# A four-tap convolution over tokens, moved from VectorE to TensorE's diagonal matrices in the first image

## The chip, the core and the metric

The kernel runs on one core of a Trainium2 chip, in fp32 throughout. The metric is the device time of one execution in microseconds. A profile belongs to one execution of its own. Engines are named as the profile names them: PE is TensorE's matrix multiplication, PEld its weight load, DVE is VectorE, ACT is ScalarE, POOL is GpSimd, and SP is SyncE, which here issues most of the transfers.

## The reference, cut to what matters

Four images of 384 channels and 48 x 48 tokens pass through four layers with residuals: a Mamba block, a patch-wise frequency filter with a depthwise convolution, an 11 x 11 depthwise convolution, and a mixture of four experts. The change touches the first layer alone:

```python
xz = xs @ in_proj_w.T
xin, z = jnp.split(xz, 2, axis=-1)
xc = jnp.pad(xin.transpose(0, 2, 1), ((0, 0), (0, 0), (D_CONV - 1, 0)))   # D_CONV = 4
xc = jax.lax.conv_general_dilated(xc, conv_w[:, None, :], (1,), 'VALID', ...)  # one filter per channel
xin = jax.nn.silu((xc + conv_b[None, :, None]).transpose(0, 2, 1))
...
h_new = dA * h_prev + dBx        # for 768 channels x 16 states, token after token
y_t = jnp.einsum('bds,bs->bd', h_new, C_t)
```

Each of the 768 inner channels has its own four weights: a token's value is the weighted sum of itself and the three tokens before it. That sum, `xc`, is what the change makes in another way. The scan of `h_new` follows.

## The kernel before

**Chunks and slots.** An image's 2304 tokens are cut into five chunks of 460 or 464 tokens (0 to 4), and the 768 channels into six row tiles of 128 partitions. One chunk of scans is 96 slots: three pairs of row tiles, and in each pair 16 states for both tiles. In each slot POOL multiplies `u` and `B` into `bu` (L831), ACT makes the decay `da` as an exponential (L820), DVE runs the scan (L844), and the result is multiplied by `C`, by DVE in two slots of three (L864) and by POOL in the third (L873). PE transposes the product with the identity and sums it in a bank `y` (L770), ACT keeps the last column as `carry` (L858). Decays are made two slots ahead of their scan, `bu` three, in small buffers (two banks for `da`, three buffers for `bu`, six for `g`).

**The order of the work.** Each engine carries out its own instructions in the order in which they were written. That order is set when the kernel is built, by a planner in slots: every other piece of work of the first layer is a task, a generator that yields the engine it wants next, and `plan` gives each task the slot from which it may go (`put(45 + 3 * j, ("x", more, j), ...)` for the projections of the next chunk). A task moves on when its slot has come, its needs are ended and a bank of the ring of three PSUM banks (`ring`) is free. Nothing of this is decided on the chip, so an instruction that waits holds up all that stands behind it on its engine.

**The projection.** `project(i, j)` makes row tile `j` of the next chunk: PE multiplies three blocks of the input projection into a bank `pin` (L642), with three columns of tokens from the chunk before it ahead of its own (the halo). ACT writes `xc` from `pin`, with the fourth weight as scale and the bias `cb` (L655). DVE adds the other three taps from the bank in three instructions (L661), and the bank is released. `project_z` makes the gate's part `pinz` in the same manner (L674, ACT copy L682). `gates` waits for all six tiles of both, loads another activation table and applies the silu to the whole of `xc` and `zs` (L693, L696), loads the first table back (L548), and `expand` (`pdbl`, L708) follows on PE. `steps` makes the time steps (`pdt` L734, ACT L744 to L747, DVE L750).

**What lies around it.** In the slots of the first image only the first layer works. From the second image on, the later layers of the image before it are tasks of other lanes and fill PE and DVE too. Ahead of the slots stands a setup: constants and weights, group norm statistics of the first image, `fold` (ACT scales the projection's weights by the norm, L591; PE makes their bias, `pbias` L598), and the first chunk's projections.

Of the kernel before, what the change touches and what calls it, by code (L numbers as in the profile page):

```python
# [9 lines left out]
F32 = mybir.dt.float32  # L10
AF = mybir.ActivationFunctionType
# [5 lines left out]
P = 128  # L17
# [4 lines left out]
DI, DS, DTR, DCONV = 768, 16, 24, 4  # L22
MT = DI // P
CHUNKS = (460, 460, 460, 460, 464)
TM = max(CHUNKS)
# [108 lines left out]
def wait(slots):  # L134
    for _ in range(slots):
        yield ("pool",)
# [3 lines left out]
def tile_layers(ctx: ExitStack, tc: tile.TileContext, a: dict, out: bass.AP):  # L140
    nc = tc.nc
# [6 lines left out]
    def const(name, shape, src, eng=None):  # L148
        t = cp.tile(shape, F32, name=name)
        (eng or nc.sync).dma_start(t, src)  # L150
        return t

    def per_channel(ap):
        tail = "abcd"[: len(ap.shape) - 1]
        tail = " ".join(tail)
        return ap.rearrange(f"(m p) {tail} -> p m {tail}", p=P)
# [4 lines left out]
    ident = const("ident", [P, P], a["c_ident"])  # L161
# [251 lines left out]
    with ExitStack() as first:  # L413
# [4 lines left out]
        def weight(name, shape, src):  # L418
            t = wp.tile(shape, F32, name=name)
            nc.scalar.dma_start(t, src)  # L420
            return t
# [4 lines left out]
        conv_w = weight("conv_w", [P, MT, DCONV], per_channel(a["L0_conv_w"]))  # L426
# [45 lines left out]
        with (  # L472
# [4 lines left out]
            for ct in range(CT):  # L477
                t = pp.tile([P, HW], F32, name=f"x0_{ct}")
# [58 lines left out]
        NC = len(CHUNKS)  # L537
# [14 lines left out]
        def now(steps):  # L552
            for _ in steps:
                pass

        def scans(wk, mm, ring, meter, place, lanes, begin):
# [5 lines left out]
            LEN = PAIR * (MT // 2)  # L562
# [19 lines left out]
            def fold(b, which):  # L582
                w = (w_inx, w_inz)[which]
                d = batch[b]
                nc.sync.dma_start(
                    w, per_channel(a["L0_in_proj_wT"])[:, :, bass.ts(which, DI)]
                )
                yield from wait(5)
                for k in range(CT):
                    yield ("act",)  # L590
                    nc.scalar.activation(  # L591
                        w[:, k, :], w[:, k, :], AF.Copy, scale=rstd0[:, b, k : k + 1]
                    )
                yield ("pe", 0, (ring, 1))
                ps, r = ring.take(f"pbias{b}_{which}")
                for j in range(MT):
                    for k in range(CT):
                        nc.tensor.matmul(  # L598
                            ps[:, j : j + 1],
                            lhsT=w[:, k, bass.ts(j, P)],  # L600
                            rhs=mean0[:, b, k : k + 1],
                            start=k == 0,
                            stop=k == CT - 1,
                        )
                yield ("dve",)
                nwm = d["nwm", which] = small.tile(
                    [P, MT], F32, name=f"nwm{b}_{which}", tag=f"nwm{which}"
                )
                nc.vector.tensor_scalar_mul(nwm, ps[:, :MT], -1.0)
                if which == 0:  # L610
                    wm = d["wm"] = small.tile([P, MT], F32, name=f"wm{b}", tag="wm")
                    nc.vector.tensor_copy(wm, ps[:, :MT])
                    cb = d["cb"] = small.tile([P, MT], F32, name=f"cb{b}", tag="cb")
                    nc.vector.tensor_tensor(cb, conv_s, nwm, ALU.mult)
                    nc.vector.tensor_tensor(cb, cb, conv_b, ALU.add)
                ring.done(r)
# [14 lines left out]
            def project(i, j):  # L631

                (b, t), c = G[i], st[i]
                n, d = CHUNKS[t], batch[b]
                halo = DCONV - 1
                lo = 0 if t else halo
                yield ("pe", 2.3, (ring, 1))
                if "xc" not in c:
                    c["xc"] = wk.tile([P, MT, TM], F32, name=f"xc{b}_{t}", tag="xc")
                ps, r = ring.take(f"pin{b}_{t}_{j}")  # L640
                for k in range(CT):
                    nc.tensor.matmul(  # L642
                        ps[:, lo : halo + n],
                        lhsT=w_inx[:, k, bass.ts(j, P)],
                        rhs=c["x"][:, k, lo : halo + n],
                        start=k == 0,
                        stop=k == CT - 1,
                    )
                yield ("act",)
                if t == 0:  # L650
                    nc.scalar.activation(
                        ps[:, :halo], nil[:, :halo], AF.Identity, bias=d["wm"][:, j : j + 1]
                    )
                acc = c["xc"][:, j, :n]
                nc.scalar.activation(  # L655
                    acc, ps[:, halo : halo + n], AF.Identity,
                    bias=d["cb"][:, j : j + 1], scale=conv_w[:, j, halo : halo + 1],
                )
                yield ("dve",)
                for k in range(halo):  # L660
                    nc.vector.scalar_tensor_tensor(  # L661
                        acc, ps[:, k : k + n], conv_w[:, j, k : k + 1], acc, ALU.mult, ALU.add
                    )
                ring.done(r)
# [159 lines left out]
            def drive(u):  # L824
                i, p, m, s, _ = where(u)
                (b, t), c = G[i], st[i]
                n = CHUNKS[t]
                bu = live["bu", u] = wk.tile(
                    [P, TM], F32, name=f"bu{b}_{t}_{m}_{s}", tag="bu", bufs=3
                )  # L830
                nc.gpsimd.tensor_mul(  # L831
                    bu[:, :n], c["u", p][:, m % 2, :n], live["B", u // 2][:, :n]
                )
# [139 lines left out]
                nc.sync.dma_start(x1d[b][bass.ts(ct, P), bass.ds(starts[t], n)], x)  # L973

            aux = Lane(1 << 30, meter, bound=False)
            named = {}

            def plan(i, at):
# [58 lines left out]
            def ready(u):  # L1037
# [3 lines left out]
                while task and not task.ended:  # L1041
# [3 lines left out]
                    n += 1  # L1045
                    assert n < 1000, "stuck"

            now(fold(0, 0))
            now(fold(0, 1))
            now(load(0))  # L1050
            for j in range(MT):
                now(project(0, j))
# [4 lines left out]
            with tc.manual_schedule():  # L1057
                ordered[0] = True
                for k in range(3):
                    spread(k, 0)  # L1060
                    spread(k, 1)
                for u in range(3):
                    drive(u)
                spread(3, 0)
                for u in range(2):
                    decay(u)
                for u in range(N + 6):
                    if u % LEN == 0 and u <= N:
                        plan(u // LEN, u)
                    if u < N and u % (LEN * NC) == 42 and u > 42:  # L1070
                        begin(G[u // LEN][0])
                    place[0] = u
                    for lane in (aux, *lanes):
                        lane.step(True, u)
                    for h, e in ((1, u - 4), (0, u - 5)):
                        if 0 < e < N and e % PAIR == PAIR - 1:
                            collect(e, h)
                    if u < N:
                        scan(u)


                    meter.slot(0.44)
                    early = u % PAIR >= 8
                    if early:
                        add(u - 5, True)
                        add(u - 3, False)
                    for lane in (aux, *lanes):
                        lane.step(False, u)
                    if u < N:
                        product_now(u)  # L1090
                    if u + 2 < N:
                        decay(u + 2)
                    if 0 < u <= N:
                        product(u - 1)
                    if u + 3 < N:
                        ready(u + 3)
                        drive(u + 3)
                    if not early:
                        add(u - 5, True)
                        add(u - 3, False)  # L1100
                    if u % 2:
                        spread((u + 7) // 2, 0)
                        spread((u + 5) // 2, 1)

                at = u
                while aux.queue or aux.active:
                    at += 1
                    meter.slot(0.0)
                    for act in (True, False):
                        for lane in (aux, *lanes):  # L1110
                            lane.step(act, at)
                lanes[0].drain(at, lanes[1:])
                place[0] = at
                ordered[0] = False
# [653 lines left out]
        ring, accr = psum("mm", 3), psum("acc", 1)  # L1768
# [167 lines left out]
```

## Time and profile before

| what | value |
|---|---|
| time, median of 3 runs | 5467.04 us (5466.89 to 5471.5) |
| the profiled execution's own time | 5472.59 us |
| its span | 5470.3 us |
| granted TensorE clock, mean | 0.912 |
| busy over the span: PE | 4689.8 us (86%) |
| DVE | 4176.4 us (76%) |
| ACT | 2999.9 us (55%) |
| POOL | 3124.6 us (57%) |
| L642 `pin`, PE, whole span | 720 records, 332.5 us |
| L844 scans, DVE, row with 1008 records | 1182.5 us, 1173 ns each |

A row of the profile names a line, an engine, an operation, what it writes and reads, its count and its busy time; then the time the engine sat idle just before it and what ended that wait. The shares are means over the whole span, in which stages with different limits follow each other: the slots of the first image fill about the first fifth, and from about 4600 us on PE works nearly alone. In a timeline a line begins with the start and the duration in microseconds. Durations of instructions that follow each other overlap by a little, so what a group costs its engine is read from start to start.

### The profile page before, as it was taken

How to read it: one execution, taken by the hardware profiler on the slowest of the kernel's cores; microseconds unless marked ns; L12 is line 12 of the kernel's file. 1: busy time of each engine (PE TensorE's matmuls, PEld its weight loads, DVE VectorE, ACT ScalarE, POOL GpSimd, SP SyncE). 2: the span in 40 equal slices, each digit the busy share in tenths (PEclk: the TensorE clock that was granted, in tenths of full speed). 3: DMA queues.
4: the chain of work that ended last, by engine and by line, in shares of the span. 5: the costliest groups of instructions: out<-in, count | busy, mean ns of one | idle time of the engine just before them, and what ended most of it. 6: DMA issues, size and time to landing. Idle time of an engine off the chain costs nothing. (4 is left out here: it accounts for less than half of the span.)

```text
span 5470.3 us, 82006 instructions
## 1 busy us (share of the span) xinstructions
PE 4689.8 (86%) x27796; PEld 3688.4 (67%) x27796; DVE 4176.4 (76%) x5806; ACT 2999.9 (55%) x6632; POOL 3124.6 (57%) x2795
## 2 busy tenths in 40 slices
PE   5677677777678989988899999988899999999899
PEld 3445445454447767665678887665678878888799
DVE  5889989999898898899988788899988774443200
ACT  3555555565458765655467655665566753334321
POOL 3878878865567777665567667665666662000000
PEclk8788888798789999999899999999999999999899
DMA  4445445454345555544566566554556564543200
GB/s 121 135 137 147 124 128 146 128 149 124 104 125 148 151 160 163 172 140 140 152 169 174 155 166 175 153 154 130 164 158 169 163 175 145 148 138 102 66 27 23
DMA packets 628393, 758.97 MB, mean 139 GB/s; under 512 B 58869, under 2 KB 622181, under 8 KB 627582
## 3 DMA queue, kind: packets, MB, share of 16 engines
q1 hardware_dynamic: 617668, 751.98, 48.5%
q8 instruction: 221, 3.62, 0.3%
q10 hardware_dynamic: 10298, 1.67, 0.2%
q14 instruction: 206, 1.69, 0.1%
HBM read 663.81 MB, written 89.65 MB: 138 GB/s over the span
## 5 line engine op out<-in xcount | busy, mean ns | idle before, releaser
L831 POOL TENSOR_TENSOR bu<-u,B 128x460 f32<-128x460 f32 (+1 forms) x1920 | 2226.4, 1168 | 1118.2 <-DVE g L844 506.7
L820 ACT ACTIVATE da<-dt,a_neg 128x460 f32<-128x460 f32 (+1 forms) x1920 | 1243.7, 649 | 317.3 <-DVE g L864 223.0
L770 PE MATMUL y<-ident,g 128*115 128x128 f32 (+1 forms) x7680 | 1169.0, 295 | 273.4 <-DVE g L864 202.0
L770 PEld LDWEIGHTS y<-ident,g 128*115 128x115 f32 (+1 forms) x7680 | 1024.1, 185 | 546.9 <-DVE g L864 246.8
L844 DVE TENSOR_TENSOR_SCAN da<-da,carry,bu 128x460 f32<-128x460 f32 (+1 forms) x1008 | 1182.5, 1173 | 69.9 <-ACT da L820 48.7
L873 POOL TENSOR_TENSOR g<-g,C 128x460 f32<-128x460 f32 (+1 forms) x660 | 767.7, 1163 | 197.9 <-ACT carry L858 195.9
L864 DVE TENSOR_TENSOR g<-da,C 128x460 f32<-128x460 f32 (+1 forms) x1260 | 796.4, 632 | 87.1 <-DMA C<-bcd 28.1
L844 DVE TENSOR_TENSOR_SCAN g<-da,carry,bu 128x460 f32<-128x460 f32 (+1 forms) x528 | 616.8, 1168 | 105.6 <-ACT da L820 61.1
L858 ACT COPY carry<-da 128x1 f32<-128x1 f32 x1008 | 159.0, 158 | 948.1 <-DVE g L864 944.8
L1601 PE MATMUL pout<-hr,we 128*128 128x144 f32 x3456 | 488.9, 298 | 49.7 <-ACT hr L1617 30.5
L1601 PEld LDWEIGHTS pout<-hr,we 128*128 128x128 f32 x3456 | 461.1, 199 | 70.2 <-ACT hr L1617 40.6
L1601 PE MATMUL ph<-xe,we 128*128 128x144 f32 x3456 | 471.1, 292 | 15.2 <-DMA xe<-x3d 10.1
L1601 PEld LDWEIGHTS ph<-xe,we 128*128 128x128 f32 x3456 | 448.6, 195 | 30.4 <-DMA xe<-x3d 8.9
L1408 PE MATMUL pc<-band,row 128*128 128x162 f32 (+14 forms) x3456 | 456.2, 285 | 7.1 <-ACT row L1395 7.1
L1408 PEld LDWEIGHTS pc<-band,row 128*128 128x128 f32 x3456 | 443.5, 195 | 11.0 <-ACT row L1395 8.3
L642 PE MATMUL pin<-xch,w_inx 128*128 128x463 f32 (+2 forms) x720 | 332.5, 602 | 33.4 <-DMA xch<-in_x 20.0
L1266 DVE SCALAR_TENSOR_TENSOR dw<-pad,w_dw,dw 128x384 f32<-128x384 f32 x576 | 347.6, 614 | 17.4 <-ACT pad L1241 6.5
L915 PE MATMUL po<-w_out,zs 128*115 128x384 f32 (+1 forms) x960 | 342.4, 497 | 9.3 <-DVE dt L750 7.8
L674 PE MATMUL pinz<-xch,w_inz 128*128 128x460 f32 (+1 forms) x720 | 326.3, 592 | 0.3 <-DVE ye L1633 0.3
L1617 ACT ACTIVATE hr<-ph,nb 128x144 f32<-128x144 f32 x576 | 176.2, 376 | 268.2 <-PE ph L1601 267.8
L844 DVE TENSOR_TENSOR_SCAN da<-da,nil,bu 128x460 f32<-128x460 f32 x252 | 294.8, 1170 | 12.8 <-ACT carry L858 8.5
L1375 ACT ACTIVATE rep<-x,br,wr 128x192 f32<-128x192 f32 x576 | 274.1, 540 | 21.0 <-DVE br L1345 20.9
(202 smaller groups left out, 5725.4 us busy)
## 6 DMA issues: line engine op xcount, KB each, us to landing
B<-bcd SPq DMA_DIRECT2D x768, 230.0 KB, 3.5
C<-bcd SPq DMA_DIRECT2D x768, 230.0 KB, 3.8
B<-bcd SPq DMA_DIRECT2D x192, 232.0 KB, 3.7
C<-bcd SPq DMA_DIRECT2D x192, 232.0 KB, 4.0
xe<-x3d SPq DMA_DIRECT2D x192, 216.0 KB, 2.9
ye<-y3d SPq DMA_DIRECT2D x144, 216.0 KB, 2.8
y3d<-ye SPq DMA_DIRECT2D x96, 216.0 KB, 2.2
xs<-x1d SPq DMA_DIRECT2D x24, 576.0 KB, 4.9
```

The costliest lines, as they stand in the source:

```text
L642: nc.tensor.matmul(ps[:, lo : halo + n], lhsT=w_inx[:, k, bass.ts(j, P)], rhs=c["x"][:, k, lo : halo + n], start=k == 0, stop=k == CT - 1,)
L674: nc.tensor.matmul(ps[:, :n], lhsT=w_inz[:, k, bass.ts(j, P)], rhs=c["x"][:, k, DCONV - 1 : DCONV - 1 + n], start=k == 0, stop=k == CT - 1,)
L770: nc.tensor.matmul(c["y", m][:w, bass.ts(k, P)], lhsT=src[:, bass.ts(k, w)], rhs=ident, is_transpose=True, start=c["terms", m] == 1 and k ...
L820: nc.scalar.activation(da[:, :n], c["dt", p][:, m % 2, :n], AF.Exp, scale=a_neg[:, m, s : s + 1])
L831: nc.gpsimd.tensor_mul(bu[:, :n], c["u", p][:, m % 2, :n], live["B", u // 2][:, :n])
L844: nc.vector.tensor_tensor_scan(here[:, :n], da[:, :n], bu[:, :n], last if t else nil[:, 0:1], ALU.mult, ALU.add,)
L864: nc.vector.tensor_mul(live["g", u][:, :n], live["h", u][:, :n], live["C", u // 2][:, :n])
L873: nc.gpsimd.tensor_mul(g[:, :n], g[:, :n], live["C", u // 2][:, :n])
L915: nc.tensor.matmul(ps[:w, :C], lhsT=c["zs"][:, m, bass.ts(k, w)], rhs=w_out0[:, m, :], start=m == 0, stop=m == MT - 1,)
L1266: nc.vector.scalar_tensor_tensor(v, src, w_dw[:, ct, k : k + 1], v, ALU.mult, ALU.add)
L1408: nc.tensor.matmul(d["acc2"][0][:, : BANDS[k] * W].rearrange("p (h w) -> p h w", w=W)[:, lo - edges[k] : hi - edges[k], xlo:xhi], lhsT=d[" ...
L1601: nc.tensor.matmul(ps[:, bass.ts(m, EB)], lhsT=w[:, k, bass.ts(m, P)], rhs=of[:, k, :], start=k == 0, stop=k == CT - 1,)
```

## The change

In chunks 1 to 4 of the first image the convolution is made by PE. Ahead of the setup's folds, ACT makes 24 diagonal matrices (six row tiles, four taps) from the identity and `conv_w`. In `project`, ACT copies the bank `pin` with its halo into a row in SBUF in place of writing `xc`, and the bank is released. A second bank is taken, PE multiplies the row, shifted by zero to three tokens, with the four diagonal matrices and sums in that bank, and ACT writes `xc` from it with the bias. DVE's three instructions are gone there. Chunk 0 of the first image and all chunks of the other images are as before; at the slot where the second image begins the pool with the matrices is released.

```diff
                 yield ("act",)
+                if taps and t:
+                    pool, diag = taps
+                    row = pool.tile([P, halo + TM], F32, name=f"row{b}_{t}_{j}", tag="row")
+                    nc.scalar.copy(row[:, : halo + n], ps[:, : halo + n])
+                    ring.done(r)
+                    yield ("pe", 3.1, (ring, 1))
+                    ps, r = ring.take(f"pcv{b}_{t}_{j}")
+                    for k in range(DCONV):
+                        nc.tensor.matmul(
+                            ps[:, :n],
+                            lhsT=diag[:, j, k, :],
+                            rhs=row[:, k : k + n],
+                            start=k == 0,
+                            stop=k == halo,
+                        )
+                    yield ("act",)
+                    nc.scalar.activation(
+                        c["xc"][:, j, :n], ps[:, :n], AF.Identity, bias=d["cb"][:, j : j + 1]
+                    )
+                    ring.done(r)
+                    return
                 if t == 0:
...
+            taps = []
...
+            first_image = ExitStack()
+            pool = first_image.enter_context(tc.tile_pool(name="taps", bufs=2))
+            diag = pool.tile([P, MT, DCONV, P], F32, name="diag", bufs=1)
+            for j in range(MT):
+                for k in range(DCONV):
+                    nc.scalar.activation(
+                        diag[:, j, k, :], ident, AF.Copy, scale=conv_w[:, j, k : k + 1]
+                    )
+            taps[:] = pool, diag
             now(fold(0, 0))
...
                 for u in range(N + 6):
+                    if u == LEN * NC:
+                        first_image.close()
+                        taps.clear()
```

## The prediction

> **What bounds the kernel now.** I read the page first, then busy time by stretch, then the waits and the timelines around the change. On the page the rows of tenths matter: one digit is 5470.3 / 40 = 136.8 us, so the first image's scans (about 90 to 1030 us) are digits 1 to 8.
>
> ```profile
> PE   5677677777678989988899999988899999999899
> ...
> DVE  5889989999898898899988788899988774443200
> ...
> L642 PE MATMUL pin<-xch,w_inx 128*128 128x463 f32 (+2 forms) x720 | 332.5, 602 | 33.4 <-DMA xch<-in_x 20.0
> ```
>
> From the second digit on DVE is at 8 to 9 tenths there and PE at 6 or 7, so over the image DVE binds and PE seems to have room. L642 gives a count: 20 chunks x 6 row tiles x 3 matmuls are 360, yet 720 records stand there: an fp32 matmul is two records.
>
> An average is not enough, because the convolution is made in one part of each chunk, from slot 45 to the gates (L693) at slot 64. In the trace this stretch lasts from the first `pin` to the table load ahead of L693: 161 to 208, 351 to 398, 538 to 585 and 726 to 776 us. Busy time by stretch (PE, PEld, DVE, ACT, POOL):
>
> ```profile
> 161.00:208.00 47.00, 35.06 (x140) 21.53 (x140) 44.90 (x58) 24.93 (x57) 33.78 (x31) 0.88 0.42 121
> 351.00:398.00 47.00, 32.94 (x140) 19.94 (x139) 44.84 (x58) 25.08 (x56) 33.99 (x31) 0.90 0.43 129
> 538.00:585.00 47.00, 33.34 (x140) 20.37 (x140) 44.60 (x57) 24.77 (x55) 33.57 (x30) 0.94 0.46 130
> 726.00:776.00 50.00, 38.68 (x164) 23.59 (x164) 45.63 (x64) 24.97 (x56) 34.32 (x32) 0.88 0.39 106
> ```
>
> DVE is full here (44.8 of 47), PE has 33 to 35. So PE's room is 12 to 14 us a stretch. The waits from 350 to 400 us show who holds whom:
>
> ```profile
> ACT carry L858 <- DVE g L864: 13.5, 9, 3.1
> ...
> PE y L770 <- DVE g L864: 5.9, 3, 2.9
> ...
> PE pin L642 <- DMA xch<-in_x: 2.3, 1, 2.3
> ```
>
> ACT and PE wait for DVE. Prices come from the timelines of PE, ACT and DVE in this stretch (start, duration):
>
> ```profile
> 350.65 4.10 PE L642 MATMUL pin<-xch,w_inx 128*128 128x463 f32 x6 [2.31 <-DMA xch<-in_x]
> ...
> 376.56 2.50 PE L642 MATMUL pin<-xch,w_inx 128*128 128x463 f32 x6
> 378.90 1.03 PE L770 MATMUL y<-ident,g 128*115 128x128 f32 x8
> ...
> 401.45 4.24 PE L708 MATMUL pdbl<-xc,w_x 128*57 128x460 f32 x6 [9.83 <-ACT xc L693]
> ```
> ```profile
> 384.99 2.13 DVE L661 SCALAR_TENSOR_TENSOR xc<-pin,conv_w,xc 128x460 f32<-128x460 f32 x3
> 387.04 1.17 DVE L844 TENSOR_TENSOR_SCAN da<-da,carry,bu 128x460 f32<-128x460 f32 x1
> ```
> ```profile
> 389.75 0.71 ACT L655 ACTIVATE xc<-pin,cb,conv_w 128x460 f32<-128x460 f32 x1
> ...
> 397.60 1.28 ACT L693 ACT_TABLE_LOAD   x1
> ```
>
> From start to start, six `pin` records cost 378.90 - 376.56 = 2.34 us (0.39 a record), a set of four transposes 0.43, and the three DVE taps 387.04 - 384.99 = 2.05.
>
> **What the Trainium skill says.** "TensorE: Matmul & The Clock Gate", Part 1: the array's clock is halved after an idle window of about 3.4 us and comes back after a busy one. The trace agrees: after waiting 9.83 us six `pdbl` records took 4.24, against 2.50 for six `pin` records when warm. The same page, "Architectural detail": ACT's queue is strictly in order. Here ACT waited up to 1.6 us for `pin` while later decays (L820) stood behind. "ScalarE: Activation LUTs", "What ACT_TABLE_LOAD costs": 186 ns + 0.833 ns a column, 93 ns more for each per-partition operand, back to back 93 ns less. L655 has two such operands: 186 + 186 + 383 = 755 ns, and the trace has 710 to 730.
>
> **The change, part by part.** The order of instructions of the two builds differs only in the first image and at the start; on SP nothing moves, so no DMA is added or moved.
>
> 1. *DVE*: 24 projections (chunks 1 to 4, six each) lose their three taps: 24 x 2.05 = 49.2 us, 12.3 a stretch. The stretch then holds some 33 us of DVE work.
>
> 2. *PE*: 24 x 4 matmuls of 460 columns, 8 records each projection at 0.39: 3.1 us, 18.6 a stretch, 74 in all. That is above PE's room of 12 to 14. For the second stretch I added PE's own work from start to start, waits left out, from 350.65 to the last transposes before `pcv` of row tile 5: six `pin` 15.7 (the first, half cold, 3.94), two `pinz` 4.6, `pdt` 1.7, 19 transposes 8.6: 30.6. With `pcv` 49.2, so the last `pcv` ends at 399.9 at the earliest. ACT then makes `xc` and two decays with their carries, 2.2 us, and loads the table at 402.1 where it did at 397.60: **+4.5 us** with no PE wait at all. PE's order is fixed, and the gates need all six row tiles: DVE's free time cannot be used before PE is through.
>
> 3. *Added waits*. `xc` now waits on ACT for `pcv`, and behind it stand the decays that DVE's next scans need; PE waits for ACT's copy before `pcv`. I followed the new order by hand with the durations above. ACT reaches `xc` of row tile 0 at 361.1 (PE is busy with `pinz`, then `pcv`), so the next decay lands at 362.4, half a microsecond later than now, in spite of the freed DVE. From then on DVE waits for ACT and ACT for PE. PE itself waits twice: `pin` of tile 3 takes the bank of `pdt`, free after the DVE reads it at L750, and that comes after `xc` of tile 2 and the Exp and Ln on ACT (2.0 us); `pcv` of tile 3 waits some 0.4 for its copy. Together about 2.1 us more: the table load comes **6.6 us later**. The copies (463 columns, nearest row L682's 0.64) are 24 x 0.64 = 15 us on ACT, which is at 25 of 47: they cost only through this order. From below these waits cost 0; from above I allow 4 us.
>
> 4. *Gates onward*. Now PE is idle 9.83 us and makes `pdbl` cold. With the lag it idles about 5, so it may stay warm; up to 1.2 us return, I take 0.7.
>
> 5. *Other stretches*. The first and third are like the second (47 us, same counts). The fourth has the group norm of the next image among its matmuls, and DVE already waits 2.1 us for PE there: from 725.83 PE's own work is 35 to 37, with six `pcv` of 464 columns (18.8) 54 to 56, then 2.4 on ACT: 782 to 784 for 775.54, with waits +8. Sum: 3 x 6.6 + 8 - 4 x 0.7 = **+25**; from below 3 x 4.5 + 6.2 - 4 x 1.2 = +15; from above, four more microseconds a stretch than the lower waits, +36.
>
> 6. *Diagonals*. 24 ACT copies of 128 columns with one per-partition scale: 186 + 93 + 107 - 93 = 0.29 us each (estimate from the ScalarE page; L439, 128x96 with none, took 0.28 alone, so 0.22 to 0.31). Six lie in idle time before or between the two Abs of L520; 18 stand between L520 (30.74 us) and L591, which starts at 33.62 when its weights land. They end near 36.8. From L591 the path runs through `pbias` and `pin` on PE without a gap, so this is **+3.2** (1.8 to 4).
>
> Everything after slot 480 keeps its order, and slides.
>
> Sum: 25 + 3 = +28 us on the profiled execution's 5472.59 (span 5470.3 and 2.3 around it), 5500.6. That execution lies 5.6 above the median of the runs, 5467.04; the same step on the median gives **5495 us**.
>
> **The rivals.**
> - *Faster: DVE's work is what counts.* If PE's extra work fits beside the scans, each stretch shrinks by up to 12.3 and the sum is -49 + 3: 5421. For it: DVE 44.8 of 47, every wait names DVE. Against: 49 us of PE work must end before the gates. It decides once PE's work from `pin` to the last `pcv` is under about 44 us, that is if `pcv` costs less than 2.3 us a projection instead of 3.1.
> - *A wash.* PE at the lower bound (no waits of its own), the first `pin` warm (1.6 back) and `pdbl` warm (1.2): 4.5 - 2.8 is under 2 a stretch, some 3.5 in the fourth, with the diagonals +11 or less: up to 5478. Against: 2.3 us of waiting for `xch` precede the first `pin`, and it is slow in all four stretches.
> - *Slower still: PE's clock.* In stretch one, `pin` of tile 5 took 3.89 instead of 2.50. If the granted clock stays near 0.88 rather than 1.0 while PE has 49 us to do, each stretch gains another 49.2 / 0.88 - 49.2 = 6.7 us: 5522. Against: the same set was warm in the other three stretches, and a busier PE idles less.
> - *Not what it says*: the new order shows four `pcv` matmuls for each of 24 projections, the taps gone there and left elsewhere. Excluded.
>
> **How the numbers follow.** A run of this kernel can tell about 0.2%, 11 us, from no change. Mechanism of the sum: 0.73; slower still 0.10; a wash 0.08; faster 0.09. The sum's own bounds are +15 + 2 and +36 + 4: 5484 to 5507. Eight times in ten needs a little of both neighbours: 5478 to 5511. Slower 0.83, within 0.2% 0.08, faster 0.09.
>
> **What would show it.** Right: DVE in the four stretches falls from 44.8 to about 33 busy while the stretches grow to some 53 us; PE is over 48 busy in them; new waits of ACT `xc` for PE `pcv`, several microseconds a stretch; the wait of PE `pdbl` for the silu falls from 9.8 to about 5; L591 starts near 36.8. Wrong: stretches of 40 us or less, `pcv` records below 0.3 us, or PE waiting for DVE in them as before.

## The result, and the profile after

| | before | after |
|---|---|---|
| time, median of 6 runs each | 5468.33 us (5466.89 to 5471.5) | 5510.3 us (5489.38 to 5511.96) |
| span of the profiled execution | 5470.3 us | 5509.6 us |
| granted TensorE clock, mean | 0.912 | 0.913 |

The change makes the kernel slower: the ratio is 1.0073, with an interval of 1.0063 to 1.0083, or 42 us, which is under 1%. The forecast was +28. The 42 fall into two parts. Up to slot 480, where the second image begins, the profiled execution after lies 29.2 us behind the one before, in the main for the reasons that the prediction gave. In the rest of the program, where no instruction is changed, 10 us more are lost between the two profiled executions (spans 39.3 apart) and 13 by the medians, and the prediction had 0 there.

The page after, rows of tenths (one digit is now 137.7 us) and the group of the projection's matmuls; the last line is the group of the new matmuls, from 160 to 900 us, both shapes together (busy and mean; then the idle time before them and what ended it):

```profile
PE   5787787787768989988889999988899999999899
...
DVE  5888778898898888889988788899988774443200
...
L642 PE MATMUL pin<-xch,w_inx 128*128 128x463 f32 (+2 forms) x720 | 328.3, 595 | 23.7 <-DMA xch<-in_x 16.1
```
```profile
L658 PE MATMUL pcv<-row,diag 128*128 128x460 f32 (+1 forms) x192 | 79.2, 555 | 4.8 <-ACT row L653 4.8
```

In the first image's digits (2 to 8) DVE falls from 8 or 9 to 7 or 8 and PE rises from 6 or 7 to 7 or 8. The new group has 192 records, 24 projections of 8. Busy time in the four stretches after (PE, PEld, DVE, ACT, POOL, then the clock):

```profile
165.03:216.59 51.56, 49.29 (x188) 28.59 (x188) 34.88 (x41) 27.51 (x65) 35.98 (x33) 1.00 0.38 111
358.57:411.79 53.22, 50.96 (x188) 29.29 (x188) 33.61 (x39) 26.59 (x62) 34.80 (x31) 0.97 0.38 115
553.82:606.90 53.08, 50.82 (x188) 29.22 (x188) 33.70 (x39) 26.67 (x62) 34.76 (x31) 0.97 0.39 116
748.32:802.50 54.18, 53.53 (x212) 31.33 (x212) 33.11 (x45) 26.62 (x63) 35.29 (x32) 0.97 0.36 100
```

DVE lost 10 to 12 us in each, and PE is now the full engine: 50.96 of 53.22 in the second. DVE idles for 53.22 - 33.61 = 19.6 us. The waits of the second stretch (waiter, engine waited for, us in total, times, longest) show who holds whom now:

```profile
ACT xc L666 <- PE pcv L658: 11.3, 6, 2.6
...
ACT row L653 <- PE pin L642: 7.4, 5, 1.7
...
DVE da L865 <- ACT carry L879: 6.4, 4, 2.6
DVE da L865 <- ACT da L841: 5.0, 4, 1.8
```

Before, ACT and PE waited for DVE. Now ACT waits for PE, six times for `pcv`, and DVE waits for what stands behind that on ACT: carries and decays. From the timelines of PE and of ACT in the same stretch (start, duration):

```profile
365.87 3.25 PE L658 MATMUL pcv<-row,diag 128*128 128x460 f32 x8
368.95 0.60 PE L791 MATMUL y<-ident,g 128*115 128x128 f32 x4
...
393.40 3.36 PE L658 MATMUL pcv<-row,diag 128*128 128x460 f32 x8 [1.62 <-ACT row L653]
...
409.67 1.47 PE L791 MATMUL y<-ident,g 128*115 128x128 f32 x12
415.64 4.85 PE L729 MATMUL pdbl<-xc,w_x 128*57 128x460 f32 x6 [4.49 <-ACT xc L714]
```
```profile
411.79 1.28 ACT L714 ACT_TABLE_LOAD   x1
```

A `pcv` set costs PE 368.95 - 365.87 = 3.08 us. Within the stretch PE has one wait of any size, 1.62 for a row copy, and the table load follows its last `pcv` by 2.1 us. The gates come when PE is through.

### The profile page after: what moved, and what is told of

It is laid out like the page before. It is cut to its first block, busy times and chain, and to the rows that moved or that the text cites. A ratio compares the mean times of both kernels' runs of the same rounds, so it can differ in the third digit from the quotient of the medians.

```text
span 5509.6 us, 82358 instructions
## 1 busy us (share of the span) xinstructions
PE 4770.5 (87%) x27988; PEld 3732.0 (68%) x27988; DVE 4132.1 (75%) x5734; ACT 3012.5 (55%) x6680; POOL 3125.3 (57%) x2795
## 5 line engine op out<-in xcount | busy, mean ns | idle before, releaser
L642 PE MATMUL pin<-xch,w_inx 128*128 128x463 f32 (+2 forms) x720 | 328.3, 595 | 23.7 <-DMA xch<-in_x 16.1
```

Source lines behind the costliest of these rows:

```text
L642: nc.tensor.matmul(ps[:, lo : halo + n], lhsT=w_inx[:, k, bass.ts(j, P)], rhs=c["x"][:, k, lo : halo + n], start=k == 0, stop=k == CT - 1,)
```

## The experiments

Each kernel ran 5 to 14 times, in five rounds beside the one before (19 to 30 runs). The measures are these. The *stretch* is the time from the first `pin` to the table load ahead of the silu, as the mean of four (before 47.7, after 53.0). The *shift* is how much later than before the scan of slot 480 starts. Both come from one profiled execution, the ratios and differences of medians from all runs. What the difference of medians has beyond the shift is called the *rest*; it joins many runs with one execution's shift, and is good to 5 to 10 us only (for e5 the ratio on record, 1.0026, is 14 us and the medians differ by 9.0). The *tail* is the same for the profiled execution alone: how much longer than in before's profile the time from the scan of slot 480 to the end is.

| kernel | stretch | shift | median against before | rest | tail, profiled | ratio |
|---|---|---|---|---|---|---|
| after | 53.0 | +29.2 | +42.0 | +12.8 | +10.1 | 1.0073 [1.0063, 1.0083] |
| e1_diag_only | 47.8 | -0.4 | +1.0 | +1.4 | -3.3 | 1.0007 [0.9998, 1.0015] |
| e2_diag_in_slots | 53.3 | +27.8 | +37.3 | +9.5 | +16.1 | 1.0063 [1.0050, 1.0076] |
| e4_one_tap | 43.0 | -16.6 | +1.9 | +18.5 | +9.4 | 1.0003 [0.9994, 1.0012] |
| e10_two_tap | 44.8 | -9.5 | +3.7 | +13.2 | -4.8 | 1.0004 [0.9995, 1.0012] |
| e6_bf16_taps | 43.0 | -13.5 | -3.8 | +9.7 | +9.8 | 0.9988 [0.9980, 0.9997] |
| e3_half | 50.4 | +13.7 | +21.6 | +7.9 | +16.5 | 1.0037 [1.0025, 1.0050] |
| e5_half_late | 48.1 | +0.9 | +9.0 | +8.1 | -3.6 | 1.0026 [1.0016, 1.0036] |
| e7_bf16_late | 42.8 | -13.6 | -5.2 | +8.4 | +16.7 | 0.9992 [0.9981, 1.0003] |
| e9_full_late | 56.0 | +33.0 | +44.6 | +11.6 | +9.9 | 1.0076 [1.0060, 1.0092] |
| e11_copy_only | 56.0 | +35.2 | +43.6 | +8.4 | -11.3 | 1.0078 [1.0065, 1.0091] |
| e8_setup_delay | 47.8 | +31.8 | +26.4 | -5.4 | -2.4 | 1.0051 [1.0038, 1.0064] |
| e12_pe_stream | 47.8 | +37.2 | +46.7 | +9.5 | -2.6 | 1.0085 [1.0072, 1.0098] |

### The two parts of the change apart

**e1_diag_only** keeps the diagonals and leaves the convolution on DVE.

```diff
-            taps[:] = pool, diag
```

> The kernel before with the 24 diagonal matrices built ahead of the folds and never used; the convolution stays on DVE everywhere. Theory (the matrices delay the setup's path, nothing else): the first scan comes 4.5 us later, as with the change, and the whole run takes 4 to 5 us more, about 5473. Rival (the 10 us which the changed kernel lost after the first image, where the order of the work is the same, come from any shift in time and not from the convolution): 5480 or more.

The first scan came 2.7 us later than before, but by slot 144 the delay was gone; the time is not to be told from before's (the interval of the ratio allows -1 to +8 us). So little of the 42 us is the diagonals' own work.

**e2_diag_in_slots** keeps the convolution on PE and makes the diagonals in a task of the slots.

```diff
+            def diagonals():
+                for j in range(MT):
+                    yield ("act",)
+                    for k in range(DCONV):
+                        nc.scalar.activation(taps[1][:, j, k, :], ident, AF.Copy, scale=conv_w[:, j, k : k + 1])
...
+                    put(6, "diag", diagonals)
```

> The changed kernel with the matrices built in slots 6 to 12 of the first chunk, where ACT has idle time, in place of ahead of the folds. Theory: the first scan is where it was before the change, the four stretches stay at +4 to +8 us each, 25 us in all; 4.5 us less than the changed kernel, about 5506. Rival (building them costs ACT the same wherever it stands): 5510.

The setup is as before (first scan 0.5 us earlier), and of after's 42.0 us 37.3 remain; e2's five runs lie between 5500 and 5517, so that the 4.7 between the two can't be told from nothing. The loss is, nearly all of it, the convolution's move.

### How much PE work the stretch takes

**e4_one_tap** leaves only the tap of the token itself, with one matmul.

```diff
-                    for k in range(DCONV):
+                    for k in (halo,):
```

> The changed kernel with one of the four diagonal matmuls in place of four: three taps are left out of the sum in chunks 1 to 4 of the first image. All copies, banks and waits are as in the changed kernel; PE's added work falls from 18.6 to 4.7 us a stretch. Theory (PE's work decides): PE has 35 us before the last tile, DVE and POOL 34 each, a stretch takes 38 to 40 us, 8 less than before, and the run about 5440. Rival (copies and waits in the fixed order decide): the stretch stays at 50 or more, 5485 and up.

Its second stretch, by busy time:

```profile
343.24:386.16 42.92, 37.35 (x152) 22.43 (x152) 33.42 (x39) 26.61 (x61) 33.49 (x30) 0.96 0.46 142
```

Copy, second bank and both reads by ACT are there as in after; only PE's work is smaller, 37.35 for 50.96. The stretch is 10.3 us shorter than after's and 4.0 shorter than before's. So the bank and the copies are not what makes after slow, and DVE's freed time is worth something once PE is out of the way. I had expected more, though: stretches of 38 to 40 and a run of about 5440. By the medians the whole run is no faster than before's.

**e10_two_tap** is the point between, on e2: taps 0 and 3, the other two are left out.

```diff
-                    for k in range(DCONV):
+                    for k in (0, halo):
```

> Two of the four fp32 diagonal matmuls (taps 0 and 3), matrices built in slots: two taps are left out of the sum in chunks 1 to 4 of the first image. PE's added work is 9.3 us a stretch, as in the half, but DVE has none of the taps. Theory (a stretch lengthens by some 3.3 us for each 4.7 us of PE work put between ACT's copy and ACT's read, from 43.0 at one tap to 53.0 at four): 46 to 47 us a stretch, level with the kernel before, which puts the break-even at about 1.6 us of PE work a projection and not at the 2.3 of the prediction. Rival (PE's room alone, 42.3 us): 42 to 43, as with one tap.

One, two and four taps give stretches of 43.0, 44.8 and 53.0; 44.8 lies under the 46 to 47 of my theory and over the 42 to 43 of the rival. From one to two, 4.65 us more PE work (six times 0.78) lengthens the stretch by 1.8; from two to four, 9.3 us lengthen it by 8.2, nearly one for one. By the prediction's sum for the second stretch PE's own work and ACT's 2.4 come to 42.3 with two taps and 51.6 with four, and that stretch took 44.98 and 53.22: there PE sets it, with some 2 us of waits on top. With one tap the sum would be 37.7, and it took 42.92: there something else sets it, and the runs don't show what. On the line between two and four taps the 47.7 of before is met at 1.55 + 1.55 x (47.7 - 44.8) / (53.0 - 44.8) = 2.1 us of PE work a projection, an estimate from two points; the change has 3.1. That holds for the stretch. The whole run with two taps is, by the medians, not faster than before's.

**e6_bf16_taps** has all four taps at a quarter of PE's price: row and matrices of e2 in bf16, so these products are rounded.

```diff
-                    row = pool.tile([P, halo + TM], F32, ...)
+                    row = pool.tile([P, halo + TM], mybir.dt.bfloat16, ...)
...
-            diag = pool.tile([P, MT, DCONV, P], F32, ...)
+            diag = pool.tile([P, MT, DCONV, P], mybir.dt.bfloat16, ...)
```

> The changed kernel with the row and the diagonal matrices in bf16, matrices built in slots: one record a matmul in place of two at half the rate, so four taps should cost PE about 0.8 us a projection, as the one tap did. The convolution's inputs are rounded to bf16 in chunks 1 to 4 of the first image. Theory (PE's work between ACT's copy and ACT's read decides): the same as with one tap, first image 15 us shorter than before and the run about 5470. Rival (the number of matmuls counts, not their length): first image as long as before or longer, 5490.

Stretch and PE's busy time (37.00 in the second) are those of one fp32 tap, as expected. It is the one version whose interval lies under before's time, by 3.8 us in the medians (e7, below, has 5.2 with an interval that takes in no change). In the profiled execution 13.5 stood at slot 480, so most of the gain is lost later.

### The order in which ACT reads

**e3_half** makes tiles 0, 2 and 4 on PE and leaves 1, 3 and 5 on DVE (on e2), so that neither engine is full.

```diff
-                if taps and t:
+                if taps and t and j % 2 == 0:
...
-                for j in range(MT):
+                for j in range(0, MT, 2):
```

> Row tiles 0, 2 and 4 are made by PE, tiles 1, 3 and 5 stay on DVE; the 12 matrices are built in slots. Theory (PE's added work against its room in the stretch decides): PE has 30.6 + 9.3 = 40 us before the last tile, DVE 41, so a stretch of 47 us shrinks by about 5 and the run takes 20 us less than before, about 5448. Rival (the waits added on ACT and DVE's order decide, not the amount of PE work): half of the loss remains, 5480.

**e5_half_late** lets ACT's reading of `pcv` stand two slots later in ACT's order.

```diff
+                    yield from wait(2)
                     yield ("act",)
```

> As the half (row tiles 0, 2, 4 on PE), but ACT reads the bank of the convolution two slots later in its order, so that it need not stand and wait for PE while the next decays stand behind it. Revised theory (the in-order waits of ACT for PE carry the loss in the half, since PE had idle time there): the second stretch falls from 51 us to 42 to 44, under the 47 of the kernel before, and the run comes to 5455 to 5470. Rival (PE's work and its clock decide in every form): no change from the half, 5490.

The second stretch of e3, then of e5, by busy time:

```profile
357.01:407.98 50.97, 43.33 (x164) 25.33 (x164) 39.07 (x48) 25.44 (x58) 33.50 (x30) 0.93 0.40 119
```
```profile
348.37:395.62 47.25, 41.51 (x164) 24.59 (x164) 39.03 (x48) 25.50 (x58) 33.59 (x30) 0.97 0.43 129
```

In e3 no engine is over 43.4 of 51, and still the stretch is longer than before's: the 20 us that I had expected to gain became a loss of 21.6. Its waits (e3, second stretch) name the order:

```profile
ACT xc L666 <- PE pcv L658: 6.2, 3, 2.9
```

Three instructions of ACT wait 6.2 us for their matmuls, and the decays stand behind them. In e5 that wait is no longer among the first of the list, and the second stretch is 3.7 us shorter with the same records on PE and DVE (2.3 in the mean of four, since the fourth grew by 1.5). PE also had the better clock there (0.97 for 0.93, 1.8 us less busy), so the order's own share of the 3.7 is not settled. But I had expected 42 to 44 and a run of 5455 to 5470, and got 47.25 and 5479: what keeps the stretch there is open.

**e9_full_late** does the same with all six tiles, **e7_bf16_late** by one slot with bf16.

```diff
+                    yield from wait(2)      # e9, on e2; e7 on e6: wait(1)
                     yield ("act",)
```

> All six row tiles with four fp32 diagonal matmuls, matrices built in slots, and ACT's read of the bank two slots later. Theory (two terms: PE's own work, and ACT's in-order waits for it): PE's work is left, 49.2 us before the last tile and 2.4 after it, so the stretches are 51 to 52 us, not 53, and the run still 5495 to 5505. Rival (the waits alone carry the loss): the stretches fall to 47 or less, as in the half with late reads, and the run to 5480.

> The bf16 taps with ACT's read of the bank one slot later. Theory (waits of ACT for PE): each stretch loses another 2 us, the first image is 20 to 25 us shorter than before and the run 5455 to 5465. Rival (with so little PE work nothing waits there): as the bf16 taps without it.

e9 is a miss: 56.0 where 51 to 52 were expected, against 53.3 in e2. PE had the same 188 records in the second stretch (52.42 busy, at a clock of 0.94), so reading later cost more than it saved. Its timeline of PE shows one place where it was lost, the `pin` of tile 3:

```profile
392.33 4.02 PE L642 MATMUL pin<-xch,w_inx 128*128 128x463 f32 x6 [2.44 <-DVE dt L772]
```

It waits 2.44 us until DVE has read `pdt` and a bank of the ring is free, and then runs slowly (4.02 for 2.50); in after this set starts without a wait. The late reading holds one of the three banks two slots longer, which fits, but a fourth bank was not tried. e7 does not differ from e6, where another 2 us a stretch were expected. With PE full the wait for `pcv` is, by e9, mostly a sign of PE's lateness, not its cause.

**e11_copy_only** takes the convolution back to DVE, but from the copied row: no diagonals, no second bank (its edit against e2, shortened).

```diff
-                    ps, r = ring.take(f"pcv{b}_{t}_{j}")
-                    for k in range(DCONV):
-                        nc.tensor.matmul(...)
+                    acc = c["xc"][:, j, :n]      # ACT writes it from row, scale and bias
+                    yield ("dve",)
+                    for k in range(halo):
+                        nc.vector.scalar_tensor_tensor(acc, row[:, k : k + n], conv_w[:, j, k : k + 1], acc, ...)
```

> ACT copies the bank into a row in SBUF as in the change, but the convolution is made from the row by ACT and DVE as before; no diagonal matrices, no second bank, no added PE work. Theory (the copies cost nothing by themselves): stretches of 47 to 48 us, run 5470 to 5475. Rival (the copies delay the decays behind them): 50 us or more, 5485.

It was meant to price the copies and can't, since DVE's taps became slower too (DVE is busy 53.23 of 55.67 us in the second stretch). DVE's and POOL's timelines in e11:

```profile
362.57 2.17 DVE L662 SCALAR_TENSOR_TENSOR xc<-row,conv_w,xc 128x460 f32<-128x460 f32 x3 [1.09 <-ACT carry L875]
...
370.09 3.61 DVE L662 SCALAR_TENSOR_TENSOR xc<-row,conv_w,xc 128x460 f32<-128x460 f32 x3
```
```profile
365.75 1.16 POOL L890 TENSOR_TENSOR g<-g,C 128x460 f32<-128x460 f32 x1 [3.03 <-ACT carry L875]
...
369.79 1.17 POOL L848 TENSOR_TENSOR bu<-u,B 128x460 f32<-128x460 f32 x1 [0.63 <-DVE g L861]
370.91 1.56 POOL L890 TENSOR_TENSOR g<-g,C 128x460 f32<-128x460 f32 x1
```

The first set of taps runs in POOL's pause (which ends at 365.75) and takes 2.17; the second runs while POOL works and takes 3.61, and POOL's own instruction 1.56 for 1.16. Of all 72 taps of e11, the 14 with no POOL instruction beside them took 0.70 us each, the 24 wholly beside POOL's work 1.28 to 1.49. From a bank in PSUM the set takes 2.13. e11 tells nothing of the copies; e4 does.

### The 10 to 13 us after slot 480

**e8_setup_delay** is e1 with the diagonals made five times over: a late start, slots as before.

```diff
-            for j in range(MT):
+            for j in [j for _ in range(5) for j in range(MT)]:
```

> The kernel before, with the matrices built five times over ahead of the folds and never used: everything from the folds on starts about 31 us later, nothing else changes. Theory (the further 10 to 20 us that the changed kernels lost after the first image come from where PE's clock happens to stand, and any shift can bring them): 31 us and some of those, 5505 to 5520. Rival (they come from the changed convolution itself): 5501.

**e12_pe_stream** is the kernel before with the matmuls of the first bias made six times: a late start with PE busy in it.

```diff
-                for j in range(MT):
+                for j in [j for _ in range(1 if b or which else 6) for j in range(MT)]:
```

> The kernel before, with the bias sums of the first fold (18 matmuls on PE) made six times over in the setup: 90 more matmuls in PE's instruction stream, 35 to 40 us later start of the slots, nothing else changed. Theory (the further 8 to 15 us that all kernels with a convolution on PE lose after the first image come from the longer PE stream and not from the convolution's place): the run is longer than the shift of the first scan by 8 or more. Rival (they come with the convolution in the slots): the run grows by the shift of the first scan alone, as with the delayed setup.

In e8 a delay of 32 us before the first scan stood at 31.8 at slot 480, and the median lay 26.4 behind: no rest, where I had expected one. In e12 the shift was 37.2 and the rest +9.5, as expected. By the medians, then, a shift alone does not bring the rest (e8, e1), and ten of the twelve experiments show one, two of them without a convolution on PE (e12, e11). The profiled executions don't bear that out: those of e12 and e11, each the fastest of its kernel's five runs, have no longer tail than before's, and neither have two kernels with the convolution on PE (e10, e5). The tail is longer, by 9.4 to 16.7, in seven of the thirteen, and all seven have the convolution on PE. The 78 runs of before beside the experiments spread by themselves over 23 us, from 5458.93 to 5481.76. So it stays open how much of the rest a kernel brings and how much the single execution.

Where the time goes within an execution can be told. Busy time from slot 480 on, before and then after:

```profile
1025.00:5470.00 4445.00, 3973.46 (x24686) 3202.26 (x24686) 3301.24 (x4708) 2440.29 (x5478) 2349.06 (x2101) 0.93 0.50 140
```
```profile
1054.00:5509.00 4455.00, 3986.04 (x24686) 3213.29 (x24686) 3301.78 (x4708) 2440.11 (x5478) 2349.57 (x2102) 0.93 0.48 140
```

The same 24,686 matmul records take PE 12.6 us more, while DVE, ACT and POOL agree within 0.6. The other traces say the same: in the seven with a longer tail the same records take PE 8.1 to 22.9 us more than in before's, in the other six -3.8 to +6.5, and DVE, ACT and POOL at most 2.0 in any. Two places, the same sets on PE before and after:

```profile
2607.28 4.69 PE L1601 MATMUL pout<-hr,we 128*128 128x144 f32 x18 [1.46 <-ACT hr L1617]
...
2618.71 2.37 PE L1601 MATMUL pout<-hr,we 128*128 128x144 f32 x18
```
```profile
2639.68 3.84 PE L1635 MATMUL pout<-hr,we 128*128 128x144 f32 x18 [1.46 <-ACT hr L1651]
...
2652.72 4.06 PE L1635 MATMUL pout<-hr,we 128*128 128x144 f32 x18
```

The clock granted during the second set was 1.00 before and 0.58 after; during the first it was 0.50 before and 0.63 after, so single sets go both ways and the sum decides. The difference grows in steps of 1 to 3 us, at slots near 499, 768, 1136, 1273 and 1303, with steps back of about 1 us between them; what decides at which sets PE falls back is open. The Trainium skill says in "TensorE: Matmul & The Clock Gate", Part 1, that the window that sets the clock runs freely and does not start with the kernel, so the moment at which a set falls into it would vary from run to run. That fits such sets, and the spread of before's own runs; it does not by itself say why the medians lie later in ten of the twelve experiments, and no run here tests it. Among the six runs of after one lies 21 us below the median, at 5489.38.

## Why the prediction was right, and where it missed

- **DVE's relief** (step 1): forecast 44.8 to about 33 a stretch, measured 44.84 to 33.61 in the second. Right, and worth nothing here.
- **PE's price** (step 2): forecast 3.1 a projection, measured 3.08. PE over 48 busy: 49.29 to 53.53.
- **The waits** (step 3): forecast 6.6 in each of the first three stretches, measured +4.4, +6.3 and +6.0 (51.56, 53.22 and 53.08 against 47.13, 46.95 and 47.11). The place was half right. PE did not wait for the bank of `pdt`; in each it waited once, for the row copy of tile 3, about 1.62 instead of 0.4. The first stretch lost less because its first `pin` was warm (2.60 us after a wait of 0.68, against 4.26 in the second), which was not forecast.
- **The fourth stretch** (step 5): forecast +8, measured +4.5 (54.2 against 49.7), under even the 6.2 without waits. PE's own work was mis-sized: with the six `pcv` it took 52.1 from the first `pin` to the end of the last `pcv`, not 54 to 56. In before one `pin` of this stretch ran slowly (5.00 us); after, the same one took 2.52.
- **The gates** (step 4): PE idled 4.49 as forecast (5), but the 0.7 did not come back. The six `pdbl` records of the second chunk took 4.85, against 4.24 before (granted clock 0.51 and 0.59), and those of all four chunks 17.9, against 18.2: an idle of 4.5 us left PE as cold as one of 9.8. The forecast went against what it had itself quoted, since 5 us are more than the idle window of about 3.4.
- **The diagonals** (step 6): L591 forecast near 36.8, it started at 36.11; the 18 diagonals ahead of it took 5.35 us, 0.30 each, as estimated (0.29). The first `pin` of the stretches came 3.7 later. That all of the +3.2 reaches the end was too much: e1 shows the delay taken up within the first 144 slots, and e2, without it, gains 1.4 at slot 480.

The +29.2 at slot 480 for the forecast +28 owes something to luck. The start of the first stretch brought 3.7 (forecast 3.2), the four stretches 21.2 (forecast 27.8), and what lies between and after them 4.3 (forecast -2.8, the gates' return). So the stretches came out 6.6 smaller than forecast and what lies outside them 7.6 larger, and the two cancel. What makes the 4.3 is not traced; it is not `pdbl`.

**The step that failed** is the sentence "Everything after slot 480 keeps its order, and slides". The order is kept, but the same records took 12.6 us more of PE. That term was put at 0 with no bound; it measures +10 in the profiled execution and +13 by the medians, and nearly all of the miss (5510 for 5495) is this. The measured 5510.3 is above the sum's own bounds (5484 to 5507). The wider range, up to 5511, holds it by 0.7 us, and it was widened for the neighbouring rivals, not for this term: that too is luck.

Of the rivals, *faster* had its point of decision nearly right: 2.3 us of PE work a projection for a shorter stretch, 2.1 by the runs with fewer taps; but a shorter stretch was not enough for a faster run. *Slower still* named the clock within the stretches, where it was 0.97 to 1.00, so that is not what happened. *A wash* is out as well: the first `pin` was warm in the first stretch alone, `pdbl` took 4.1 to 4.9 us in all four, and PE had waits of its own in three.

## What to carry to other kernels

Before moving work to the engine with the lower mean share, add up that engine's own work from start to start in the very stretch that must end before the next step can begin. The gain ends where that sum, with some 2 us of waits here, passes the old length of the stretch, whatever the relieved engine does with its time. And in a program whose PE falls in and out of its full clock, the clock of untouched work later need not stay the same: between two profiled executions here that made 12.6 us, about 0.2%, more than the 3.8 us that the best version gained. A stretch won early is not yet a faster run: e4 and e10 were 17 and 10 us ahead at slot 480, and not measurably faster at the end.

## What the hardware showed that was not expected

- **DVE and POOL on SBUF.** Three DVE taps with both inputs in SBUF took 2.17 us in POOL's pause and 3.61 beside it. The Trainium skill says so in "SBUF — State Buffer", "Who interferes with whom": a DVE instruction with two SBUF inputs contends with a GpSimd instruction that reads SBUF. The trace of e11 agrees, and POOL lost too (1.56 for 1.16); I had not thought of it when e11 was made.
- **The clock of untouched work.** Identical sets of matmuls ran at different clocks in two kernels (2.37 us at a granted 1.00, 4.06 at 0.58), and over 4450 us this came to 12.6 us, though the mean granted clock was 0.912 and 0.913.
